# Spreading the second attention score over the partitions with two DMAs instead of TensorE transposes

## The chip, the cores and the metric

The kernel runs on one core of one Trainium2 chip. The metric is the device time of that core in microseconds (us), as the median of several runs. The kernel before takes 2290.54 us (median of 3 runs, 2290.47 to 2291.78). The span of the profiled execution is 2288.5 us. All times below that are given as a point ("at 1296.72") are microseconds from the start of that span.

## The reference, cut to what matters

`x` is 128 batch rows of 128 nodes by 512 features, `adj` is 128 by 128, everything is fp32. Four layers follow one another, each with a residual and a layer norm. The change is in layer 2, graph attention:

```python
h = jnp.einsum('bnc,cf->bnf', x, W)
a1, a2 = (a[:F_, 0], a[F_:, 0])
s1 = jnp.einsum('bnf,f->bn', h, a1)
s2 = jnp.einsum('bnf,f->bn', h, a2)
e = jax.nn.leaky_relu(s1[:, :, None] + s2[:, None, :], negative_slope=ALPHA)
e = e * mask[None, :, :]
att = jax.nn.softmax(e, axis=2)
h_prime = jnp.einsum('bij,bjf->bif', att, h)
return jax.nn.elu(h_prime + beta * h)
```

For one batch row, `s1` belongs to the node i that lies on the partitions, and `s2` to the node j that lies along the free dimension. So `s2`, which is computed with one value per partition, must be turned into a row that every partition can read. How this is done is what changes. The other layers (a graph convolution, a linear attention, an edge maximum) are not touched.

## The kernel before

**Groups and stages.** The 128 batch rows go through in 32 groups of four (`G = 4`). A group `g` passes through `layer0` to `layer3`. The large products (`r_y` in layer 0, `r_m` and `r_v` in layer 1, `r_z` in layer 2) are each made of seven block products in the order 1, 2, 6, 5, 7, 3, 4 (`ORDER`, line 287), which accumulate into three PSUM tiles, 0, 1 and 2 (`REGION`, line 288: blocks 1, 6, 7, 4 go to tile 0, block 2 to tile 1, blocks 5 and 3 to tile 2). After each block its partial sum is copied out or added out (`out` in `product`, lines 350 to 355), and the next block on the same PSUM tile has to wait until that reading is done. The reads of blocks 1, 2, 6, 5, 7, 3, 4 of `r_y` are the seven VectorE instructions `x<-r_y,x`.

**Order.** The order of the work is written by hand. Each piece of a group has a place in time in `TABLE` (in slots of 2.48 us; a group starts 28 slots after the one before), with exceptions for the last three groups in `LAST`. All pieces are sorted by this place (lines 730 and 731), and TensorE, VectorE, ScalarE and GpSimd issue their instructions in exactly that order, through the wrapper `InOrder`. So three or four groups at different stages are interleaved on each engine. The DMAs on SyncE are not held to the written order: the loads of `x` (`load`) and the stores of the output (`store`) are placed by a scheduler.

**The work around the change, for group g.**

- `dots` and `scale_dots` (VectorE) compute both scores into the small tile `d` of shape [128, 2, 4]: `d[:, 0, :]` is `s1`, `d[:, 1, :]` is `s2`. The last instruction of this is `d<-d,rstd`.
- `spread` (TensorE) makes four transposes of `d[:, 1, b]`, broadcast over 128 columns, into one PSUM bank, `p_s`. The place is 61.6, between block 3 and block 4 of the product `r_m` of the next group.
- `leaky` (VectorE) adds `p_s` and `s1` into `e` and then applies the leaky relu (`e<-e`). `weighted` (GpSimd) multiplies by `adj`, `greatest` (VectorE) takes the maximum, `exps` (ScalarE) the exponentials, `divide` the reciprocal of the sums on VectorE (`rs`) and the product on GpSimd (`e<-e,rs`), `turn_att` (TensorE) transposes into `p_eT`.
- On GpSimd, just ahead of `weighted`, stand the four instructions of `left_factors` that prepare the sums `s_y` for the product `r_y` of group g+2.
- On VectorE, the seven reads of `r_y` of group g+2 stand between and after these pieces.

Of the kernel before, what the change touches and what calls it, by code (L numbers as in the profile page):

```python
# [8 lines left out]
FP = mybir.dt.float32  # L9
# [20 lines left out]
def kernel(  # L30
# [31 lines left out]

    nc = tc.nc
    pe, dve, act, pool = (InOrder(tc, e) for e in (nc.tensor, nc.vector, nc.scalar, nc.gpsimd))
    B, N, D = x.shape
    P = 128
    assert N == P and D % P == 0
# [2 lines left out]
    G = 4  # L70
    NG = B // G
# [4 lines left out]
    work = ctx.enter_context(tc.tile_pool(name="work", bufs=1))  # L76
    small = ctx.enter_context(tc.tile_pool(name="small", bufs=4))
    psum = ctx.enter_context(tc.tile_pool(name="psum", bufs=4, space=bass.MemoryType.PSUM))

    def bank(name):  # L80
        return psum.tile([P, D], FP, tag="ps", name=name)
# [8 lines left out]
    x1, x2, x3 = {}, {}, {}  # L90

    def load(g):
        x1[g] = data.tile([P, G, D], FP, tag="x1", name=f"x1_{g}", bufs=3)
        if g == 0:
            for b in range(G):
                nc.sync.dma_start(x1[g][:, b, :], x[b])
        else:
            nc.sync.dma_start(x1[g], x[g * G : (g + 1) * G].rearrange("b n d -> n b d"))

    load(0)  # L100
    w0_sb = const.tile([P, K, D], FP)
    nc.scalar.dma_start(w0_sb, w0.rearrange("(k p) f -> p k f", p=P))
# [19 lines left out]
    ident = const.tile([P, P], FP)  # L122
# [99 lines left out]
    def each(at, f):  # L222
        for b in range(len(at)):
            emit(at[b], f, b)

    def row(at, step, n=G):
        return [at + i * step for i in range(n)]
# [6 lines left out]
        masked=[39.95], norms=[42.5], inverse=[43.1], v=row(42, 1, 7), attend=row(50.6, 1),  # L234
        residual=row(51.0, 1), dots=row(54.2, 1.1), norm1=[55.2], scale=[58.8],
        apply1=row(65.4, 0.33),
        spread=[61.6], leaky=[62.0], weighted=[63.4], greatest=[64.3], exps=[64.4],
        divide=[65.8], turn_att=[68.6], with_beta=[69.0], gather=row(71.5, 1),
        z_sums=row(75.3, 0.5), z_w=row(77, 1, 7), exp=[87.5, 88.5, 90.4, 92.0],
        elu=[87.8, 89.4, 92.8, 93.8], norm2=[95.0], apply2=row(95.7, 0.33),  # L240
# [10 lines left out]
            stats3=[27.0, 29.9, 32.2, 35.8], norm3=[42.0], apply3=row(44.0, 0.8), store=[47.4],  # L251
        ),
        NG - 2: dict(
            scale=[5.6], apply1=row(24.3, 0.8), spread=[6.9], leaky=[7.4], weighted=[9.0],
            greatest=[10.5], exps=[11.2], divide=[13.6], turn_att=[18.3], with_beta=[18.9],
            gather=row(36.7, 0.9), z_sums=row(39.95, 1.3),
            z_w=[40.0, 41.8, 43.5, 45.2, 47.0, 49.4, 51.1], exp=[51.5, 52.2, 56.2, 58.6],
            elu=row(56.9, 2.3), norm2=[66.1], apply2=row(67.7, 0.8), widen=row(73.0, 0.86),
# [7 lines left out]
            scale=[47.0], apply1=row(47.5, 0.8), spread=[48.9], leaky=[49.4], weighted=[51.0],  # L266
            greatest=[52.4], exps=row(53.2, 0.6), divide=row(53.9, 0.6),
            turn_att=row(54.4, 0.6), with_beta=row(54.9, 0.6), gather=[55.2, 56.1, 60.5, 65.0],
# [96 lines left out]
    def stats(s, g, b, t):  # L365
        if b == 0:
            s["mv"] = small.tile([P, G, 2], FP, tag="mv", name=f"mv_{g}", bufs=6)
        st = small.tile([P, 6], FP, tag="st", name=f"st_{g}_{b}")
        dve.bn_stats(st, t)
        dve.bn_aggr(s["mv"][:, b, :], st)  # L370

    def norm(at, apply_at, s, g, t):

        n = G // len(at)

        def spread(i):
            sl = slice(i * n, i * n + n)
            ve = small.tile([P, n], FP, tag=f"ve{n}", name=f"ve_{g}_{i}")
            dve.tensor_scalar(ve, s["mv"][:, sl, 1], EPS, None, op0=ALU.add)
            s["r", i] = small.tile([P, n], FP, tag=f"rstd{n}", name=f"rstd_{g}_{i}")  # L380
            pool.tensor_tensor(s["r", i], ve, mhalf[:, sl], ALU.pow)

        def shift(i):
            sl = slice(i * n, i * n + n)
            s["nm", i] = small.tile([P, n], FP, tag=f"nmean{n}", name=f"nmean_{g}_{i}")
            dve.scalar_tensor_tensor(
                s["nm", i], s["mv"][:, sl, 0], -1.0, s["r", i], op0=ALU.mult, op1=ALU.mult
            )

        def apply(b):  # L390
            i, j = b // n, b % n
            act.activation(
                t()[:, b, :],
                t()[:, b, :],
                AF.Identity,
                bias=s["nm", i][:, j : j + 1],
                scale=s["r", i][:, j : j + 1],
            )

        each(at, spread)  # L400
        for i in range(len(at)):
            emit(apply_at[i * n] - 0.1, shift, i)
        each(apply_at, apply)


    def layer0(g, t):
        s = {}

        def aggregate(b):
            if b == 0:  # L410
                s["yT"] = work.tile([P, K, G * P], FP, tag="aT_yz", name=f"yT_{g}")
            p = bank(f"p_y_{g}_{b}")
            for k in range(K):
                pe.matmul(
                    p[:, k * P : (k + 1) * P],
                    x1[g][:, b, k * P : (k + 1) * P],
                    adjT,
                    start=True,
                    stop=True,
                )  # L420
            act.copy(
                s["yT"][:, :, b * P : (b + 1) * P], p.rearrange("p (k n) -> p k n", k=K)
            )

        def biased(b):
            pool.tensor_tensor(x1[g][:, b, :], x1[g][:, b, :], bias_sb, ALU.add)

        if g > 0:
            emit(t["load"][0], load, g)
        each(t["y"], aggregate)  # L430
        each(t["bias"], biased)
        left_factors(t["y_sums"], s, "yT", "s_yz", f"y_{g}", 0)
        product(t["y_w"], f"y_{g}", by_rows, s, "0", rows_of(lambda: x1[g]), False)
        each(t["stats0"], lambda b: stats(s, f"0_{g}", b, x1[g][:, b, :]))
        norm(t["norm0"], t["apply0"], s, f"0_{g}", lambda: x1[g])
# [120 lines left out]
    s12 = {}  # L556
# [4 lines left out]
    def layer2(g, t):  # L561
        s = {}

        def spread():
            s["p"] = bank(f"p_s2_{g}")
            for b in range(G):
                pe.transpose(
                    s["p"][:, b * P : (b + 1) * P],
                    s12[g][:, 1, b : b + 1].to_broadcast([P, P]),
                    ident,  # L570
                )

        def leaky():
            e = work.tile([P, G, P], FP, tag="e", name=f"e_{g}")
            dve.tensor_tensor(
                e,
                s["p"].rearrange("p (b n) -> p b n", b=G),
                s12[g][:, 0, :, None].to_broadcast([P, G, P]),
                ALU.add,
            )  # L580
            dve.scalar_tensor_tensor(e, e, ALPHA, e, op0=ALU.mult, op1=ALU.max)
            s["e"] = e
# [89 lines left out]

        n = G // len(t["exps"])
        emit(t["spread"][0], spread)
        emit(t["leaky"][0], leaky)
        emit(t["weighted"][0], weighted)
        emit(t["greatest"][0], greatest)
# [16 lines left out]
    def layer3(g, t):  # L694
        s = {}

        def widen(b):
            s["a", b] = bank(f"p_a_{g}_{b}")
            pe.matmul(s["a", b], adjT, x3[g][:, b, :], start=True, stop=True)

        def top(b):
            x = x3[g][:, b, :]
            mx = small.tile([P, 1], FP, tag="mx", name=f"mx_{g}_{b}")
            dve.tensor_reduce(mx, s["a", b], AX.X, ALU.max)
            tp = small.tile([P, 1], FP, tag="top", name=f"top_{g}_{b}")
            dve.tensor_scalar(tp, mx, b3_sb, 0.0, op0=ALU.add, op1=ALU.max)
            act.activation(x, x, AF.Identity, bias=tp)

        def store(i):
            for b in range(i * n, i * n + n):  # L710
                nc.sync.dma_start(out[g * G + b], x3[g][:, b, :])

        n = G // len(t["store"])
        each(t["widen"], widen)
        each(t["top"], top)
        each(t["stats3"], lambda b: stats(s, f"3_{g}", b, x3[g][:, b, :]))
        norm(t["norm3"], t["apply3"], s, f"3_{g}", lambda: x3[g])
        each(t["store"], store)
# [8 lines left out]
    for g in range(NG):  # L727
        for layer in (layer0, layer1, layer2, layer3):
            layer(g, times(g))
# [31 lines left out]
```

## Time and profile before

| What | Value |
|---|---|
| time, median of 3 | 2290.54 us |
| span of the profiled execution | 2288.5 us |
| mean granted TensorE clock | 0.996 |
| ScalarE busy | 1005.3 us (44%) |
| GpSimd busy | 959.2 us (42%) |
| DMA moved | 75.21 MB, mean 33 GB/s |
| loads of `x`, 1024 KB each | 5.2 us from issue to landing |

The page gives for each engine how long it was busy, and then the chain of work that ended last: followed back from the last instruction, it says on which engine the time of the span was spent. The groups of instructions give busy time and the mean duration of one instruction, and after the last bar the time for which the engine sat idle just before them. The timeline lists single instructions with start and duration, and in brackets the idle time before them. Two neighbouring instructions of one engine overlap by about 0.1 us in it[...]. Since every group of the steady part runs the same list, its timeline repeats: the stretch from 1240 to 1314 us is used below as the example of all of them.

### The profile page before, as it was taken

Reading aid. Unit: us, or ns where it says so; the run is one execution under the profiler, and the core shown is the slowest. Engines: PE = TensorE matmul, PEld = TensorE weight load, DVE = VectorE, ACT = ScalarE, POOL = GpSimd, SP = SyncE. Lnnn points to the kernel's source line nnn. Section 1 sums busy time; section 2 is a strip of 40 time slices with the busy share of each in tenths; the row PEclk is TensorE's granted clock in tenths of the full one; section 3 lists DMA queues with packets and bytes.
Section 4 is the critical chain, followed back from the end, with each engine's and each line's share of the span. In section 5 each row is a group of like instructions: output and inputs, shape, how many; then the busy total and the mean of one; then the engine's idle time right before and its main releaser. Section 6 shows DMA issues by size and latency. Waiting matters only on the chain.

```text
span 2288.5 us, 31182 instructions
## 1 busy us (share of the span) xinstructions
PE 2250.7 (98%) x11809; PEld 1914.8 (84%) x11809; DVE 1577.0 (69%) x3319; ACT 1005.3 (44%) x1800; POOL 959.2 (42%) x775
## 2 busy tenths in 40 slices
PE   7999999999999999999999999999999999999996
PEld 5888888888888888888888888888888888888873
DVE  4656776666776667766667766667767677666677
ACT  2224444444444454444444444444444544444435
POOL 4434444344444334444344443444443344443422
PEclk9999999999999999999999999999999999999998
DMA  4000011100111100111100111001111001110001
GB/s 162 19 19 10 28 38 38 37 21 18 38 37 37 38 19 19 38 37 38 37 10 28 38 37 37 21 18 38 37 37 38 19 20 37 37 38 19 9 12 55
DMA packets 38886, 75.21 MB, mean 33 GB/s; under 512 B 3024, under 2 KB 3152, under 8 KB 38736
## 3 DMA queue, kind: packets, MB, share of 16 engines
q1 hardware_dynamic: 37536, 70.86, 8.7%
q10 hardware_dynamic: 1200, 2.36, 0.3%
q8 instruction: 93, 1.52, 0.3%
q14 instruction: 57, 0.47, 0.1%
HBM read 39.65 MB, written 33.55 MB: 32 GB/s over the span
## 4 chain that ended last, share of the span: by engine, by line
PE 94%; DVE 4%; POOL 1%; ACT 1%; issue 1%; DMA 0%; ACTq 0%; DVEq 0%; POOLq 0%
PE r_y L26 17%; PE r_v L26 16%; PE r_m L26 16%; PE r_z L26 16%; PE p_z L26 5%; PE p_rel L26 5%; PE p_o L26 5%; PE p_a L26 5%; PE p_y L26 5%; PE p_xT L26 2%; DVE x L26 1%; PE p_n L26 1%; DVE st L26 1%; PE p_eT L26 1%; PE p_m L26 1%; PE p_s L26 1%
## 5 line engine op out<-in xcount | busy, mean ns | idle before, releaser
L26 ACT ACTIVATE x<-x,nmean,rstd 128x512 f32<-128x512 f32 x512 | 386.4, 809 | 128.0 <-DVE nmean L26 127.9
L26 DVE BATCH_NORM_STATS2 st<-x 128x6 f32<-128x512 f32 x512 | 352.4, 688 | 75.3 <-ACT x L26 66.6
L26 POOL TENSOR_TENSOR rstd<-ve,mhalf 128x4 f32<-128x4 f32 (+1 forms) x134 | 144.5, 1078 | 245.3 <-DVE ve L26 241.3
L26 POOL TENSOR_TENSOR x<-x,bias_sb 128x512 f32<-128x512 f32 x128 | 174.8, 1368 | 145.5 <-PE p_y L26 145.5
L26 DVE SCALAR_TENSOR_TENSOR scr<-x,wa 128x512 f32<-128x512 f32 x256 | 214.9, 891 | 0.0
L26 ACT ACTIVATE x<-x,top 128x512 f32<-128x512 f32 x128 | 92.4, 722 | 254.1 <-DVE top L26 189.7
L26 DVE TENSOR_TENSOR x<-r_y,x 128x512 f32<-128x512 f32 x224 | 152.9, 683 | 54.4 <-PE r_y L26 44.5
L26 DVE TENSOR_TENSOR v<-r_v,v 128x512 f32<-128x512 f32 x96 | 65.8, 685 | 177.0 <-PE r_v L26 174.0
L26 POOL TENSOR_TENSOR s_x<-xT 128x512 f32<-128x512 f32 x64 | 82.2, 1285 | 222.2 <-ACT xT L26 222.2
L26 ACT COPY yT<-p_y 128x512 f32<-128x512 f32 x128 | 75.0, 586 | 206.0 <-PE p_y L26 206.0
L26 DVE SCALAR_TENSOR_TENSOR x<-p_o,rn,x 128x512 f32<-128x512 f32 x128 | 95.9, 749 | 99.5 <-PE p_o L26 96.5
L26 DVE SCALAR_TENSOR_TENSOR x<-m,x 128x512 f32<-128x512 f32 x128 | 115.1, 899 | 61.7 <-ACT m L26 51.3
L26 ACT COPY c<-r_z 128x512 f32<-128x512 f32 x124 | 72.6, 585 | 175.9 <-DVE scr L26 151.5
L26 PEld LDWEIGHTS p_y<-adjT,x 128*128 128x128 f32 x1024 | 135.3, 194 | 12.9 <-ACT adjT L26 5.0
L26 PEld LDWEIGHTS p_z<-eT,x 128*128 128x128 f32 x1024 | 135.4, 194 | 8.3 <-DVE x L26 1.2
L26 PE MATMUL p_y<-adjT,x 128*128 128x128 f32 x1024 | 136.1, 278 | 6.2 <-ACT adjT L26 4.7
L26 PEld LDWEIGHTS p_rel<-tT,xT 128*128 128x128 f32 x1024 | 134.2, 192 | 7.4 <-DVE tT L26 0.8
L26 PE MATMUL p_a<-x,adjT 128*128 128x512 f32 x256 | 133.6, 607 | 3.5 <-DVE mx L26 1.8
L26 PE MATMUL p_z<-eT,x 128*128 128x128 f32 x1024 | 136.4, 277 | 0.4 <-DVE x L26 0.4
L26 PE MATMUL p_rel<-tT,xT 128*128 128x128 f32 x1024 | 135.0, 275 | 0.6 <-DVE tT L26 0.6
L26 POOL TENSOR_TENSOR s_z<-zT 128x512 f32<-128x512 f32 x31 | 39.2, 1265 | 223.9 <-ACT zT L26 223.9
L26 PE MATMUL p_o<-v,rel 128*128 128x512 f32 x256 | 130.6, 594 | 0.0
(120 smaller groups left out, 5075.2 us busy)
## 6 DMA issues: line engine op xcount, KB each, us to landing
out_dram<-x SPq DMA_DIRECT2D x128, 256.0 KB, 2.0
x<-in_x_dram SPq DMA_DIRECT2D x31, 1024.0 KB, 5.2
w_sb<-in_L_gnn_weight_dram ACTq DMA_DIRECT2D x1, 1024.0 KB, 5.7
x<-in_x_dram SPq DMA_DIRECT2D x4, 256.0 KB, 7.5
wq_sb<-in_L_gnn_Wq_dram SPq DMA_DIRECT2D x1, 1024.0 KB, 11.7
wk_sb<-in_L_gnn_Wk_dram SPq DMA_DIRECT2D x1, 1024.0 KB, 14.6
w_sb<-in_L_gnn_W_dram ACTq DMA_DIRECT2D x1, 1024.0 KB, 10.2
wv_sb<-in_L_gnn_Wv_dram SPq DMA_DIRECT2D x1, 1024.0 KB, 13.7
```

The costliest lines, as they stand in the source:

```text
L26: return lambda *args, **kw: self.tc.keep_in_program_order(op(*args, **kw))
```

## The change: what it does and what it is for

For every group but the last, `spread` no longer runs on TensorE. Instead, the scores `s2` of the group (128 partitions by 4 values) are written by a DMA to a small tensor in DRAM, and a second DMA reads these 512 values back to every partition, as one row of 2 KB each, into the SBUF tile `wide`. `leaky` then reads this tile instead of the PSUM bank. The row holds the values with the node outside and the batch row inside (`p n b`), and `leaky` reads it as `p b n`, so along the node the reading steps over 4 values (16 bytes). The aim is to take the four transposes off TensorE. In the last group the transposes stay.

Both DMAs are issued by SyncE. All DMAs in the loop that SyncE issues (loads, the two new ones, stores) are now issued in the written order. The place of `spread` moves forward to 58.9, right behind `scale_dots` (58.8). In the group before the last (`NG - 2`) `leaky` and the pieces after it are placed later.

```diff
+    sync = InOrder(tc, nc.sync)
...
+    dram = ctx.enter_context(tc.tile_pool(name="dram", bufs=2, space=bass.MemoryType.DRAM))
...
-            nc.sync.dma_start(x1[g], x[g * G : (g + 1) * G].rearrange("b n d -> n b d"))
+            sync.dma_start(x1[g], x[g * G : (g + 1) * G].rearrange("b n d -> n b d"))
...
-        spread=[61.6], leaky=[62.0], weighted=[63.4], greatest=[64.3], exps=[64.4],
+        spread=[58.9], leaky=[62.0], weighted=[63.4], greatest=[64.3], exps=[64.4],
...
-            scale=[5.6], apply1=row(24.3, 0.8), spread=[6.9], leaky=[7.4], weighted=[9.0],
-            greatest=[10.5], exps=[11.2], divide=[13.6], turn_att=[18.3], with_beta=[18.9],
+            scale=[5.6], apply1=row(24.3, 0.8), spread=[5.7], leaky=[11.5], weighted=[13.1],
+            greatest=[14.5], exps=[15.2], divide=[17.6], turn_att=[20.9], with_beta=[21.5],
...
         def spread():
-            s["p"] = bank(f"p_s2_{g}")
-            for b in range(G):
-                pe.transpose(
-                    s["p"][:, b * P : (b + 1) * P],
-                    s12[g][:, 1, b : b + 1].to_broadcast([P, P]),
-                    ident,
-                )
+            if g == NG - 1:
...
+            else:
+                row = dram.tile([P, G], FP, tag="s2", name=f"s2d_{g}")
+                sync.dma_start(row, s12[g][:, 1, :])
+                wide = work.tile([P, P, G], FP, tag="s2", name=f"s2_{g}")
+                sync.dma_start(
+                    wide.rearrange("p n b -> p (n b)"),
+                    row.rearrange("n b -> (n b)")[None, :].to_broadcast([P, P * G]),
+                )
+                s["s2"] = wide.rearrange("p n b -> p b n")
...
             dve.tensor_tensor(
                 e,
-                s["p"].rearrange("p (b n) -> p b n", b=G),
+                s["s2"],
                 s12[g][:, 0, :, None].to_broadcast([P, G, P]),
                 ALU.add,
             )
...
-                nc.sync.dma_start(out[g * G + b], x3[g][:, b, :])
+                sync.dma_start(out[g * G + b], x3[g][:, b, :])
```

More of the change, by code (lines that the diff above doesn't have):

```diff
@@ L564, in spread @@
         def spread():
-            s["p"] = bank(f"p_s2_{g}")
-            for b in range(G):
-                pe.transpose(
-                    s["p"][:, b * P : (b + 1) * P],
-                    s12[g][:, 1, b : b + 1].to_broadcast([P, P]),
-                    ident,
+            if g == NG - 1:
+                p = bank(f"p_s2_{g}")
+                for b in range(G):
+                    pe.transpose(
+                        p[:, b * P : (b + 1) * P],
+                        s12[g][:, 1, b : b + 1].to_broadcast([P, P]),
+                        ident,
+                    )
+                s["s2"] = p.rearrange("p (b n) -> p b n", b=G)
+            else:
[5 more added lines that the diff above has]
+                    row.rearrange("n b -> (n b)")[None, :].to_broadcast([P, P * G]),
                 )
+                s["s2"] = wide.rearrange("p n b -> p b n")
         def leaky():
```

## The prediction

> **What bounds the kernel now.** I read the busy shares first, then the chain of work that ended last, then the groups that the change touches, and then one period of the timeline engine by engine.
>
> ```profile
> PE 2250.7 (98%) x11809; PEld 1914.8 (84%) x11809; DVE 1577.0 (69%) x3319; ACT 1005.3 (44%) x1800; POOL 959.2 (42%) x775
> ...
> PE 94%; DVE 4%; POOL 1%; ACT 1%; issue 1%; DMA 0%; ACTq 0%; DVEq 0%; POOLq 0%
> ...
> L26 PE MATMUL p_s<-ident,d 128*128 128x128 f32 x128 | 19.3, 273 | 2.1 <-DVE d L26 2.1
> ...
> L26 DVE TENSOR_TENSOR e<-p_s,d 128x512 f32<-128x512 f32 x32 | 21.8, 682 | 1.4 <-PE p_s L26 1.4
> ...
> out_dram<-x SPq DMA_DIRECT2D x128, 256.0 KB, 2.0
> ```
>
> TensorE is busy for 98% of the span and holds 94% of the chain: in the steady part it has no gap, so time taken off it is gained, provided that no other engine then makes it wait. The removed transposes wait for nothing in the steady part (the 2.1 us are one wait, in group 0). TensorE's timeline prices them and shows the block of `r_y` that will matter:
>
> ```profile
> 1293.76 0.60 PE L26 MATMUL p_s<-ident,d 128*128 128x128 f32 x4
> 1294.20 1.89 PE L26 MATMUL r_m<-xT,t_m 128*128 128x256 f32 x8
> ...
> 1310.30 1.89 PE L26 MATMUL r_y<-t,yT 128*128 128x256 f32 x8
> ```
>
> The next block starts 0.44 us after the transposes: that is their price. The last line is block 4 of `r_y`. It may start once VectorE has read block 7 from the same PSUM tile. VectorE and GpSimd in the same stretch:
>
> ```profile
> 1286.84 0.17 DVE L26 TENSOR_TENSOR d<-d,rstd 128x8 f32<-128x8 f32 x1
> ...
> 1296.72 0.68 DVE L26 TENSOR_TENSOR e<-p_s,d 128x512 f32<-128x512 f32 x1
> 1297.44 0.77 DVE L26 SCALAR_TENSOR_TENSOR e<-e 128x512 f32<-128x512 f32 x1
> 1298.13 0.68 DVE L26 TENSOR_TENSOR x<-r_y,x 128x512 f32<-128x512 f32 x1
> 1299.59 0.69 DVE L26 TENSOR_REDUCE nm<-e 128x4 f32<-128x512 f32 x1 [0.78 <-POOL e L26]
> ...
> 1308.68 0.69 DVE L26 TENSOR_TENSOR x<-r_y,x 128x512 f32<-128x512 f32 x1
> ```
> ```profile
> 1296.38 1.28 POOL L26 TENSOR_TENSOR s_y<-yT,s_y 128x512 f32<-128x512 f32 x1
> ...
> 1306.41 1.04 POOL L26 TENSOR_TENSOR e<-e,rs 128x512 f32<-128x512 f32 x1 [6.85 <-DVE rs L26]
> 1307.56 1.02 POOL L26 TENSOR_TENSOR rstd<-ve,mhalf 128x4 f32<-128x4 f32 x1
> ```
>
> VectorE is 69% busy on average, but from 1296 to 1309 it is full. The read of block 7 ends at 1308.68 + 0.69 = 1309.37, and block 4 starts at 1310.30: 0.93 us of room. I take 0.1 us from a VectorE end to the start of a TensorE block that waited for it: in group 0 a read ends at 122.64 and `r_y` starts at 122.79, while other waits show about 0.06. Also, `e` is added while GpSimd runs the last `s_y` sum, 1296.38 to 1297.66. I looked at this overlap in twelve periods from 185 to 2130 us; it is the same each time.
>
> **What the Trainium skill says.** (1) "SBUF — State Buffer", section "Who interferes with whom": a VectorE instruction with two SBUF inputs contends with a GpSimd instruction that reads SBUF; whichever starts first holds the shared port and the other is fully blocked, while a VectorE instruction with at most one SBUF input doesn't contend. This trace agrees. In group 0, a tensor_tensor on two SBUF inputs, 0.69 us when alone, meets a GpSimd instruction that ends at 116.56, and itself ends at 117.12, 0.56 later:
>
> ```profile
> 115.30 1.26 POOL L26 TENSOR_TENSOR yT<-yT 128x512 f32<-128x512 f32 x1
> ```
> ```profile
> 115.89 1.23 DVE L26 TENSOR_TENSOR t<-w_sb 128x512 f32<-128x512 f32 x1
> ```
>
> `d<-d,rstd`, whose second input is a broadcast, took 1.24 us instead of 0.17 in group 0, beside such a sum, and `e<-p_s,d`, with one input in PSUM, stays at 680 to 692 ns in all 32 cases. (2) The same page, "Door 1: The DMA port swizzle", notes that SBUF has lines of 16 bytes and that each access which crosses to a new line pays a penalty. It gives no figure, and the trace shows no large VectorE read of that kind. (3) "DMA: Bandwidth & Descriptors", "Anatomy of one DMA": about 2.0 us of fixed cost. The 256 KB stores land in 2.0 us, so this case agrees.
>
> **The change part by part.**
>
> *Removed from TensorE*: 31 x 4 transposes at 0.44 us for four, 13.6 us in all. In group 0 nothing is gained: TensorE stood there until 115.51 for `d`, and block 4 of `r_m` after it needs VectorE's read of block 7, which runs until 115.96. Group 30 lies in the tail, where TensorE already waits for others. So 29 groups x 0.44 = 12.8 us to be gained.
>
> *Added DMAs*: the write moves 2 KB in pieces of 16 bytes, the read 256 KB. Neither shape is in the trace. Lower bound: the 2.0 us of the stores for each, plus 0.4 us of issue (a DMA instruction takes 0.39 on SyncE), 4.8 us. Upper: for the first load of 64 KB 2.4 us were measured; twice 3 us and issue give 7. I take 5. From the end of `d` (1287.01) to `e` there are 9.7 us, so in the steady part it is hidden. In group 0 `e` starts 5.26 us after `d` ends (115.37 to 120.63): 0 to 2 us of waiting, I take 0.3.
>
> *SyncE in written order*: per group the four stores of g-2 (52.5 slots), the two new DMAs (58.9), the load of g+3 (64). The stores were issued at 1268.41 to 1272.95, before `d`. Behind the pair stands the load, issued at 1277.36 until now and some 12 us later then, but its first reader comes 20 slots, 50 us, later. The cost is nothing.
>
> *`e` reads SBUF instead of PSUM.* Now both inputs are in SBUF, and the last `s_y` sum, which started 0.34 us earlier, holds the port. By the pattern above `e` ends 0.56 after GpSimd, 1297.66 + 0.56 = 1298.22 instead of 1297.40. The next instruction `e<-e` then runs free in 0.69 instead of 0.77, so the first read of `r_y` starts at 1298.87 instead of 1298.13: **0.74 us late**. Nothing downstream gives this back: `nm<-e` waits for GpSimd's `e`, which is as late; then VectorE is full up to the reciprocal, on which GpSimd's `e<-e,rs`, then `rstd`, then `nmean`, then the read of block 7 hang.
>
> *The 16-byte step.* Bounds: 0, or every element takes twice as long. From `eT` with 128x512 (680 ns) and with 128x128 (292 ns), 384 elements cost 388 ns, so 512 cost 0.52 us more. I take the upper end, since every single element lies in a new line. VectorE is then 0.74 + 0.52 = 1.26 us late.
>
> *What that does to block 4.* It can start at 1309.37 + delay + 0.1, and a block after a wait loses about 0.1 more (2.00 instead of 1.89 us after the wait at 2210.11). Before, it started at 1310.30. So a period changes by delay - 0.73 us, never below -0.44. With 1.26: +0.53 us. Earlier blocks also wait (block 6: the read ends at 1300.07, the block would be due at 1299.83), but the last wait contains these.
>
> *Sum*: 29 x 0.53 = +15.4; group 0: 0.3 of waiting plus 0.52 for the slow read, +0.8, since `r_y` already waits there for this VectorE chain (0.43 us); tail: -0.4 for the transposes, up to +2 for `eT` placed later, I take 0. 2290.5 + 16.2 = **2306.7 us**, said as 2306.
>
> **The rivals.**
>
> A. *The port lock alone, the step of 16 bytes is free.* Delay 0.74, period +0.01: the gain of 0.44 is just eaten by the wait for block 7. 2290.5 + 29 x 0.01 + about 0.5 for the ends = 2291. For it: the page gives no size for the penalty. Against: a step that leaves no second access in a line is the case it warns of.
>
> B. *The gain arrives.* Neither lock nor step costs: 2290.5 - 12.8 + 0.5 = 2278. For it: TensorE at 98% without gaps, VectorE at 69%. Against: twelve equal overlaps of `e` with a GpSimd sum, and the long two-input instructions that I followed, which all end 0.56 us after GpSimd's. If only the step costs, `e` ends at 1296.72 + 1.20, the read is 0.44 late, a period gains 0.73 - 0.44 = 0.29, and it is 2283.
>
> C. *The DMA pair takes more than 9.7 us.* Then VectorE waits in every group, and each us adds as much to a period. Two DMAs at 2.0 us speak against it; at 11 us it would be about 1.3 x 29 = 38 us more than my forecast.
>
> **How the numbers follow.** Forecast (lock and step, wholly or in good part) 0.53, A 0.25, B with its variant 0.20, C 0.02. Slower by over 0.2% (above 2295.1) are the forecast and C, 0.54 with rounding; same is A, 0.26; faster is B, 0.20. The range reaches down to 2283, B's variant, and up to 2311: 0.15 us of latency instead of 0.1 (+1.5), 2 us in group 0, 2 us in the tail.
>
> **What would show it.** In the groups after, `e` from SBUF should average near 2.0 us (0.94 until the port is free, then 0.56 + 0.52); 1.5 says A, 0.7 says B. TensorE's waits should list `r_y` waiting for VectorE's `x` some 29 to 90 times, 20 us or more in all; the period, now 69.46 us, should be near 70.0. SyncE's waits should show the second DMA behind the first for about 2 us, and `e` waiting for a DMA at most in group 0. A DMA as the releaser of `e` in every group would make the prediction wrong, as would an `e` that overlaps `s_y` and takes 0.7 us.

## The result, and the profile after

The changed kernel takes **2303.55 us** (median of four runs, 2302.08 to 2304.05); the kernel before, beside it on the same chip, 2291.16 us (2290.47 to 2291.84). The ratio is **1.0053**, with a 95% interval of 1.0036 to 1.007: slower, by some 12 us. 2306 was forecast.

I read the page of the changed kernel in the same order as before: busy time of each engine, then the shares of the chain of waits, then the DMA issues (KB each, median us from issue to landing).

```profile
PE 2257.9 (98%) x11685; PEld 1908.1 (83%) x11685; DVE 1604.9 (70%) x3319; ACT 1006.1 (44%) x1800; POOL 959.9 (42%) x775
...
PE 89%; DVE 7%; POOL 1%; ACT 1%; issue 1%; DMA 1%; ACTq 0%; DVEq 0%; POOLq 0%
...
s<-s2d SPq DMA_DIRECT2D x31, 256.0 KB, 5.3
```

TensorE has 124 instructions fewer and is nevertheless "busy" for 7 us more: in the modelled busy time, short waits inside a run of matmuls don't show as gaps. Its share of the chain falls from 94% to 89%, and VectorE's rises from 4% to 7%. That is where the forecast looked for it. VectorE's group for `e` (count, then the shortest, median and longest in ns, then the first and last start):

```profile
L26 DVE TENSOR_TENSOR e<-s,d x31: 1055/1786/1796, 122.0 to 2206.9; 128x512 f32<-128x512 f32 x31
```

It was 680 to 692 ns before. The same stretch of a period as in the prediction, on GpSimd and VectorE of the changed kernel (start, duration, both in us), and last the `tT` of the kernel before, to measure from:

```profile
1304.36 1.27 POOL L26 TENSOR_TENSOR s_y<-yT,s_y 128x512 f32<-128x512 f32 x1
```
```profile
1304.12 0.66 DVE L26 TENSOR_TENSOR tT<-r_m,tT 128x512 f32<-128x512 f32 x1
1304.70 1.79 DVE L26 TENSOR_TENSOR e<-s,d 128x512 f32<-128x512 f32 x1
1306.52 0.69 DVE L26 SCALAR_TENSOR_TENSOR e<-e 128x512 f32<-128x512 f32 x1
1307.13 0.68 DVE L26 TENSOR_TENSOR x<-r_y,x 128x512 f32<-128x512 f32 x1
...
1317.62 0.16 DVE L26 SCALAR_TENSOR_TENSOR nmean<-mv,rstd 128x4 f32<-128x4 f32 x1 [1.13 <-POOL rstd L26]
1317.70 0.69 DVE L26 TENSOR_TENSOR x<-r_y,x 128x512 f32<-128x512 f32 x1
```
```profile
1296.15 0.66 DVE L26 TENSOR_TENSOR tT<-r_m,tT 128x512 f32<-128x512 f32 x1
```

`e` starts 0.34 us after the `s_y` sum and ends 0.86 us after it (1306.49 against 1305.63); in all 28 periods it is 0.86. The first read of `r_y` starts 3.01 us after `tT` started, where before it was 1.98: VectorE is **1.03 us late**. At the read of block 7 (the last line) it is still 1.05 late, 13.58 us after `tT` instead of 12.53: nothing in between gave it back. TensorE in the same stretch, and below it the kernel before:

```profile
1306.92 1.05 PE L26 MATMUL p_rel<-tT,xT 128*128 128x128 f32 x8
1307.96 1.97 PE L26 MATMUL r_y<-t,s_y 128*128 128x256 f32 x8
...
1315.00 1.05 PE L26 MATMUL p_rel<-tT,xT 128*128 128x128 f32 x8
1316.00 1.97 PE L26 MATMUL r_y<-w_sb,s_y 128*128 128x256 f32 x8
1317.80 0.60 PE L26 MATMUL p_eT<-ident,e 128*128 128x128 f32 x4
1318.44 1.99 PE L26 MATMUL r_y<-t,yT 128*128 128x256 f32 x8
```
```profile
1299.38 1.05 PE L26 MATMUL p_rel<-tT,xT 128*128 128x128 f32 x8
1300.27 1.89 PE L26 MATMUL r_y<-t,s_y 128*128 128x256 f32 x8
...
1309.86 0.60 PE L26 MATMUL p_eT<-ident,e 128*128 128x128 f32 x4
```

Three blocks of `r_y` start late, and are recognised by the start of the line before them and by their own duration. An `r_y` block follows a `p_rel` block after 0.89 us where nothing is awaited (1299.38 to 1300.27 before); the first of the three now comes after 1.04, the second after 1.00, and the last, block 4, comes 0.64 after `p_eT` instead of 0.44. Each of them then takes 1.97 to 1.99 instead of 1.89. The waits are 0.15 + 0.10 + 0.20 in the median of all groups, and by the start of what follows them the slower blocks cost 0.07 + 0.07 + 0.10: 0.70 us a period. The transposes gave 0.44, which leaves 0.26. From one `d` to the next (28 periods, groups 1 to 29) the median period went from 69.46 to 69.72 us, **+0.26**: the sum is the measured one. The average went from 69.462 to 69.749, +0.288, because two of the 28 periods are longer than the others by 0.35.

The profiled spans differ by 13.5 us (2288.5 and 2302.0). By the starts of `d`: 28 periods bring +8.04, the stretch from group 0 to group 1 +3.40 (61.33 to 64.73), and the rest from group 29 to the end +2.03 (168.11 to 170.14).

**Group 0.** Waits in brackets:

```profile
122.04 1.05 DVE L26 TENSOR_TENSOR e<-s,d 128x512 f32<-128x512 f32 x1 [1.28 <-DMA s<-s2d]
```
```profile
124.57 2.98 PE L26 MATMUL r_y<-t,s_y 128*128 128x256 f32 x8 [2.17 <-DVE x L26]
```
```profile
124.50:127.30 2.80, 2.73 (x8) 2.26 (x9) 1.35 (x3) 1.38 (x7) 0.67 (x1) 0.66 0.00 0
127.30:129.00 1.70, 1.70 (x10) 1.66 (x9) 0.78 (x2) 1.70 (x5) 0.50 (x1) 0.56 0.00 0
```

`e` waits 1.28 us for the read from DRAM. The `r_y` block behind it waits 2.17 us instead of 0.43 and then takes 2.98 us. The last fence is the table by stretch (length, busy us and instructions of the five engines, granted TensorE clock, DMA share, GB/s): over the 4.5 us after the wait the granted clock is 0.66 and 0.56 of full speed in the mean, and 0.50 from 125.4 to 128.7. That is 2.80 x 0.34 + 1.70 x 0.44 = 1.7 us lost, and with the 1.74 us of longer waiting it makes up the 3.40.

**The end** also has a longer wait with a lower clock behind it (0.50 from 2217.8 to 2224.5). No DMA is waited for here: the pieces of group 30 that the change placed later now stand ahead of `rel` on VectorE, from which GpSimd makes `sq`:

```profile
2216.93 1.16 PE L26 MATMUL p_n<-ones,sq 128*128 128x1 f32 x8 [3.01 <-POOL sq L26]
2219.67 1.11 PE L26 MATMUL p_eT<-ident,e 128*128 128x128 f32 x4 [1.59 <-POOL e L26]
```
```profile
2217.00:2220.50 3.50, 1.91 (x12) 1.83 (x13) 2.10 (x6) 0.00 (x0) 1.93 (x2) 0.61 0.02 5
2220.50:2226.00 5.50, 5.50 (x18) 4.48 (x17) 0.97 (x4) 3.99 (x6) 1.08 (x2) 0.63 0.00 0
```

### The profile page after: what moved, and what is told of

The parts are those of the page before. It is cut to its first block, busy times and chain, and to the rows that moved or that the text cites. A ratio compares the mean times of both kernels' runs of the same rounds, so it can differ in the third digit from the quotient of the medians.

```text
span 2302.0 us, 30995 instructions
## 1 busy us (share of the span) xinstructions
PE 2257.9 (98%) x11685; PEld 1908.1 (83%) x11685; DVE 1604.9 (70%) x3319; ACT 1006.1 (44%) x1800; POOL 959.9 (42%) x775
## 4 chain that ended last, share of the span: by engine, by line
PE 89%; DVE 7%; POOL 1%; ACT 1%; issue 1%; DMA 1%; ACTq 0%; DVEq 0%; POOLq 0%
PE r_v L26 16%; PE r_z L26 16%; PE r_m L26 15%; PE r_y L26 15%; PE p_z L26 5%; PE p_y L26 5%; PE p_a L26 5%; PE p_o L26 5%; PE p_rel L26 4%; DVE x L26 2%; PE p_xT L26 2%; DVE st L26 1%; PE p_n L26 1%; DVE e L26 1%; PE p_m L26 1%
```

## The experiments

The **theory**: `e` with two SBUF inputs is held by the port that GpSimd uses, and the 16-byte step of `s2` adds to it; VectorE's chain is late, and the late reads of `r_y` hold TensorE by more than the transposes gave. **Rivals**: the DMA pair, or the written order of SyncE, is what costs; or the steady part is no worse, and the ends are. Expectations are quoted as they were written ahead of each run. The first four kernels share a median of the kernel before of 2290.59 us, the last four one of 2291.56.

### 1. The row in DRAM turned, so that `e` reads packed elements

```
-row = dram.tile([P, G], ...)
-sync.dma_start(row, s12[g][:, 1, :])
-wide = work.tile([P, P, G], ...)
+row = dram.tile([G, P], ...)
+sync.dma_start(row.rearrange("b n -> n b"), s12[g][:, 1, :])
+wide = work.tile([P, G, P], ...)
...
-s["s2"] = wide.rearrange("p n b -> p b n")
+s["s2"] = wide
```

> The changed kernel, but the row in DRAM is written with the batch row outside and the node inside, so that the tile is read with neighbouring values (no 16-byte step); the write DMA then moves pieces of 4 bytes. Theory (port lock plus step plus the chain to the read of block 7): e still waits for the s_y sum, ends 0.56 us after it, so about 1.5 us long instead of 1.79; VectorE is 0.74 late instead of 1.03; the period falls from 69.72 to about 69.45 us, as long as before the change; time about 2295 us. Rival (the step costs nothing, the lock alone makes e 1.79 long): e stays at 1.79, time 2303. Rival (the DMAs cost): the write with 4-byte pieces is slower, so e waits for a DMA and the time is above 2303.

Measured: 2464.55 us, ratio 1.076 (1.0745 to 1.0775). The theory's number missed by 170 us. DMA issues, then VectorE's waits (us in all, times, longest), then the group of `e`:

```profile
s2d<-d SPq DMA_DIRECT2D x31, 2.0 KB, 8.4
```
```profile
DVE e L26 <- DMA s<-s2d: 157.5, 31, 9.6
```
```profile
L26 DVE TENSOR_TENSOR e<-s,d x31: 691/692/694, 130.2 to 2366.7; 128x512 f32<-128x512 f32 x31
```

The write now goes out in pieces of 4 bytes instead of 16, and lands in 8.4 us instead of 1.4. With the read (6.0) the pair passes the 9.7 us of room, and `e` waits in every group; the mean period is 74.77 us. This is what the prediction's rival C would have looked like, and it shows by contrast that the pair of the changed kernel, which holds `e` only in group 0, is not the cost in the steady part. The run was meant to price the step and does so in another way: `e` comes so late here that no `s_y` sum runs beside it, and it takes 0.692 us. In group 0 of the changed kernel, also with no sum beside it, it takes 1.055; in group 0 of run 8, packed and without a sum, 0.680. The 16-byte step costs 0.36 us for 512 elements, 0.71 ns each.

### 2. The read of block 7 ahead of `nmean`

```
-apply2=row(95.7, 0.33)
+apply2=row(95.85, 0.33)
```

The read no longer stands behind `nmean`, which waits for GpSimd's `rstd`.

> The changed kernel, with one place in the written order moved: VectorE's read of block 7 of r_y stands ahead of nmean of layer 2, no longer behind it, so it doesn't hang on GpSimd's e<-e,rs and rstd. Theory: the wait of block 4 (0.20 us and 0.10 of restart) goes, those of blocks 6 and 3 stay; e stays at 1.79 us; the period falls by about 0.30 to 69.42 us; time about 2295 us. Rival (what costs is the DMA pair or e itself, not the chain to block 7): unchanged, 2303.

Measured: 2295.15 us, ratio 1.0019 (1.0011 to 1.0026). `e` still takes 1.785 us, and the period is 69.42 us: 0.3 us less than in the changed kernel, for moving one read on VectorE by the length of one wait. Block 4 doesn't wait any more (0.44 after `p_eT`), while blocks 6 and 3 wait as in the changed kernel. What set the period there is this read, not `e`'s own length.

### 3. One input of `e` in PSUM again

ScalarE copies the first scores (128x4) into a PSUM tile, and `e` takes its broadcast input from there; `s2` stays in SBUF with its step.

```
+p1 = bank(f"p_s1_{g}")
+act.copy(p1[:, :G], s12[g][:, 0, :])
+s["s1"] = p1[:, :G]
...
-s12[g][:, 0, :, None].to_broadcast([P, G, P]),
+s["s1"][:, :, None].to_broadcast([P, G, P]),
```

> The changed kernel, with s1 copied by ScalarE (128x4) into a PSUM bank that the change had freed, so that e has only one input in SBUF; the step of 16 bytes stays. Theory (port lock): e no longer waits for GpSimd and takes about 1.05 us, as in the two groups where no sum runs beside it; VectorE is about 0.3 late instead of 1.03, which is less than the room that block 4 has; TensorE has no wait in the steady part and the period is 69.02 to 69.1 us; time about 2284 us. Rival (no lock, the DMA-written tile is slow to read in itself): e stays at 1.79 and the time at 2303.

Measured: 2283.13 us, ratio 0.9967 (0.9954 to 0.9979). VectorE and GpSimd of this kernel:

```profile
1293.01 1.08 DVE L26 TENSOR_TENSOR e<-s,p_s 128x512 f32<-128x512 f32 x1
```
```profile
1292.66 1.27 POOL L26 TENSOR_TENSOR s_y<-yT,s_y 128x512 f32<-128x512 f32 x1
```

The overlap is the same, but `e` runs through in 1.08 us instead of 1.79. The DMAs, the order of SyncE and the step are all still there; what went is the second SBUF input. VectorE is 0.33 us late. Without the transposes block 4 is due 0.44 earlier, so 0.93 - 0.44 = 0.49 us of its room are left, which is enough: no block of `r_y` waits, and the period is 69.03 us. Nearly the whole 0.44 of the transposes is gained. The total gains less than 29 x 0.44 because the two ends stay long (63.67 and 169.60 us).

### 4. TensorE's old work put back

Four transposes a group at the old place, in groups 0 to 29; nothing reads their result, and `e` uses the DMA's row as before.

```
+if g < NG - 2:
+    emit(28.0 * g + 61.6, idle_turns)
```

> The changed kernel with the four transposes put back at their old place in groups 0 to 29, their result unread: the DMA path and the extra TensorE work together. Theory (block 4 of r_y starts when VectorE has read block 7, not when TensorE is free): the 0.44 us of TensorE fall into waits that are there anyway; the period stays at 69.7 us within 0.1, time 2300 to 2306 us. Rival (TensorE's own work sets the period, and the loss comes from elsewhere): 29 x 0.44 us more, 2316 us.

Measured: 2303.72 us, ratio 1.0056 (1.0043 to 1.0068); mean period 69.746 us, against 69.749 in the changed kernel. Blocks 6 and 3 now start without a wait, block 4 still waits (0.16 us), and it is as late as before: 0.44 us of TensorE work a group costs nothing. In this stretch TensorE has that much slack, and the end of the stretch is VectorE's.

### 5. The ends as before

Group 0 and group 30 with the transposes at their old places and times, the DMA pair in groups 1 to 29 only.

```
-if g == NG - 1:
+if g == 0 or g >= NG - 2:
```

> The changed kernel with the old transposes, at their old places, in group 0 and in the group before the last; the DMAs stay in groups 1 to 29. Theory (the loss is the sum of a slow steady part and of two losses at the ends): the steady period stays at 69.73 us, group 0 and the tail go back to those of the kernel before: 2290.5 + 29 x 0.28 = about 2298.7 us. Rival (the ends cost nothing, all of the 13 us lies in the period): 2303.

Measured: 2298.57 us, ratio 1.0028 (1.0017 to 1.0038), so about 5 us of the loss are in the ends. The period stays at 69.73. Group 0 to 1 takes 62.34 us (64.73 after), group 29 to the end 166.1 (170.14 after).

Neither end is quite that of the kernel before, and the forecast was met partly by luck. The tail is 2 us shorter: the kernel before has a stretch of lower clock in its own tail (0.71 between 2245.38 and 2250.38 us), which this run has not, nor has run 8 (166.4 us), whose last two groups run as they do before. Group 0 is 1.0 us longer: `p_s` waits 2.09 us there, as it does before (2.10), but here the granted clock is 0.50 from 116.7 to 120.0 us, and before it is 1.00. So the same wait is followed by a lower clock in one kernel and not in the other; its length alone doesn't decide.

### 6. Runs 3 and 5 together

> The changed kernel with s1 in PSUM in groups 1 to 29 (one SBUF input, no port lock) and with the old transposes in group 0 and in the group before the last. Theory (TensorE's work is the bound once VectorE isn't late): the period is 69.03 us, the ends are those of before, and the 29 x 0.43 us arrive: about 2278 us. Rival (the DMA path costs something in each period that is not seen yet): 2281 us or more.

Measured: **2277.41 us** (2276.47 to 2277.88), ratio 0.9938 (0.9925 to 0.995): faster than the kernel before by 14 us and than the changed one by 26. Mean period 69.049 us, ends 61.34 and 165.4. 28 x 0.41 = 11.6 us of it are the steady part. The tail gives 2.7, of which some 1.7 are the lower clock in the tail of the kernel before, which isn't the change's doing. This is the change as it can be used: the gain was there, behind the port lock.

### 7. SyncE's order

Loads and stores issued as before, only the two new DMAs in written order; the load of 1 MB then stands ahead of the pair instead of 0.4 us behind it.

```
-sync.dma_start(x1[g], x[g * G : (g + 1) * G].rearrange("b n d -> n b d"))
+nc.sync.dma_start(x1[g], x[g * G : (g + 1) * G].rearrange("b n d -> n b d"))
```

(and the same for the stores)

> The changed kernel with loads and stores no longer held to the written order; only the two new DMAs are. The load of 1024 KB then stands ahead of the pair and not right behind it. Theory (the second DMA lands late, 5.3 us, because the load that is issued 0.4 us after it shares the DMA engines): it lands in 2 to 2.5 us, group 0 no longer waits for it and keeps its clock, about 3 us less in group 0; the steady period stays at 69.73; time about 2300.5 us. Rival (5.3 us is what the read to all partitions from one row costs): landing 5 us, time 2303.

Measured: 2299.95 us, ratio 1.0039 (1.0025 to 1.0053). DMA issues and group 0 of this kernel:

```profile
s<-s2d SPq DMA_DIRECT2D x31, 256.0 KB, 4.0
```
```profile
123.50 1.97 PE L26 MATMUL r_y<-t,s_y 128*128 128x256 f32 x8 [1.23 <-DVE x L26]
```
```profile
124.50:130.00 5.50, 5.50 (x35) 5.06 (x34) 2.55 (x6) 4.47 (x12) 1.04 (x1) 1.00 0.00 1
```

The read lands in 4.0 us in the median, not in the 2 to 2.5 that I expected without the load behind it: 4.0 is the read itself, and 1.3 was the load's. In group 0, `e` waits 0.31 us instead of 1.28. Less than half of this difference is the read's (4.18 us instead of 4.62). The rest is the write's (1.41 instead of 1.94), which in the changed kernel had landed before the load was issued, so the order doesn't explain it. TensorE waits 1.23 us instead of 2.17, and the granted clock stays at 1.00. Group 0 to 1 takes 62.13 us. The median period is as it was, so the order costs nothing there. The 3.6 us are 2.6 in group 0, of which 1.7 are the clock's, and about 1 of other things: this run has no long single periods (0.7) and a tail shorter by 0.4.

### 8. The lock alone

In the kernel before, ScalarE copies the transposed scores from PSUM into a packed SBUF tile, which `e` reads: two SBUF inputs, no step, no DMA, in groups 0 to 29.

```
+s["w"] = work.tile([P, G, P], ...)
+act.copy(s["w"], s["p"].rearrange("p (b n) -> p b n", b=G))
...
-s["p"].rearrange("p (b n) -> p b n", b=G),
+s["w"] if g < NG - 2 else s["p"].rearrange("p (b n) -> p b n", b=G),
```

> The kernel before, transposes included, but in groups 0 to 29 ScalarE copies the PSUM bank of the second scores into a packed SBUF tile, and e reads that: two SBUF inputs, no 16-byte step, no DMA. Theory (lock alone): e waits for the s_y sum and takes about 1.5 us instead of 0.68, VectorE is 0.74 late, which is within the 0.93 us of room that block 4 has when the transposes stay: period 69.46 to 69.5, time 2290 to 2292 us. Rival (no lock; the 16-byte step and the DMA make e long): e takes 0.69 us, time 2290.5.

Measured: 2291.14 us, ratio 1.0 (0.9992 to 1.0008).

```profile
L26 DVE TENSOR_TENSOR e<-s,d x30: 680/1476/1489, 120.9 to 2131.1; 128x512 f32<-128x512 f32 x30
```

`e` takes 1.476 us and ends 0.55 us after GpSimd's sum; VectorE is 0.72 us late, and the median period is 69.46, as without the copy. The lock alone uses up most of the 0.93 us of room and costs nothing while the transposes are there.

## Why the prediction was right, and where its terms were off

**Right, and shown.** The direction, and the way: `e` is held by the port (runs 3 and 8), VectorE's lateness passes undiminished to the read of block 7 (1.03 at the first read, 1.05 there), and that read sets the period (runs 2 and 4). The port lock was forecast as 0.74 us late and measured as 0.72. The rule that a period changes by the delay less 0.73 us, never below -0.44, holds within 0.04 us for the three delays that were measured (median periods):

| kernel | VectorE late, us | rule | period change |
|---|---|---|---|
| changed | 1.03 | +0.30 | +0.26 |
| run 3 | 0.33 | -0.40 | -0.43 |
| run 8, transposes still there | 0.72 | 0 at least | 0.00 |

It is a little high because of the 0.1 us from a VectorE end to the start of a waiting block: for block 4 it was 0.05 (1318.39 to 1318.44), for blocks 6 and 3 0.15.

The Trainium skill, "SBUF — State Buffer", "Who interferes with whom", carried this, and the runs agree on both halves of it: 1.48 us with two SBUF inputs in packed form, 1.09 us with one, the latter with the step and with the same sum beside it.

**The 16-byte step was mis-sized.** I took the upper bound, 0.52 us; it is 0.36 by itself (group 0 against run 1), and 0.31 as added delay beside the lock (1.03 - 0.72). The delay was therefore 1.03 instead of 1.26, and the steady part cost 29 x 0.29 = 8.4 us by the mean period instead of 15.4. The Trainium skill, "SBUF — State Buffer", "Door 1: The DMA port swizzle", named the penalty without a size; half way between the bounds would have been nearer.

**Group 0 was mis-sized**, +3.4 instead of +0.8, half of it longer waiting and half the lower clock. The failing step is the DMA pair: 5 us were taken, and in group 0 it took 6.6, still inside the bounds of 4.8 to 7. The write was a little faster than the 2.0 us of a store (1.94 there, 1.4 in the median), the read slower (4.62 there, 5.3 in the median): a store's 2.0 us was no price for a row that goes to 128 partitions. "The cost is nothing" of SyncE's order failed with it, if by less: the order puts the load behind the read, which adds 1.3 us to it in the median and 0.4 in group 0. That TensorE's clock can be lower after a wait, 1.7 us here, stands in no step of the prediction.

**The tail was mis-sized**, about +1.75 (the 2.03 less one longer period) instead of 0, and this is still too little: the kernel before lost some 1.7 us in its own tail to a lower clock, and against run 5, which has none, the changed kernel's tail is 4.0 us longer. The term that failed is the `eT` placed later, taken at 0 with up to 2. The waits for `sq` and `e` are 3.0 and 1.6 us, and the clock is at 0.50 for 6.7 us behind the first. How the 4.0 us divide between waits and clock isn't separated.

So 16.2 us were forecast, 15.4 of them in the steady part, and 13.5 came in the profiled span, 8.4 of them there: two errors of opposite sign. That the total came within some 3 us is in part luck. **The rivals:** A describes run 8, lock without step; the changed kernel with a free step was not tried. B's arrival is run 6. C is run 1.

**The signs.** `e` "near 2.0 us" came at 1.79, nearer to it than to the 1.5 of rival A. The first DMA holds SyncE for 1.2 us in the mean (38.3 us in 31 groups), not 2. `e` waits for a DMA once (last line below), in group 0. A poor sign was that TensorE's waits should list `r_y` waiting for `x` with 20 us or more in all (us in all, times, longest):

```profile
PEld r_y L26 <- DVE x L26: 8.5, 29, 0.6
...
PE r_y L26 <- DVE x L26: 2.8, 3, 2.2
...
DVE e L26 <- DMA s<-s2d: 1.3, 1, 1.3
```

The first line has the 29 periods but only 0.3 us each: most of the loss lies in waits of 0.1 to 0.2 us that the modelled ends of the matmuls swallow. Starts compared between two kernels show them.

**Open:** single periods that are longer than the others by 0.3 to 0.4 us (70.09 among 69.72), two in the changed kernel and one or two in six of the experiments. In the changed kernel one VectorE instruction starts 0.35 us late in each; what it waits for doesn't show. Open too is what decides whether a wait of TensorE is followed by a lower clock.

## What to carry to other kernels

When an input of a VectorE instruction moves from PSUM to SBUF, look in the timeline at what GpSimd does beside that instruction, not at its duration: here 0.4 us of saved TensorE work turned into a loss through an add that became 1.1 us longer, and one small copy to PSUM turned it back. A saved piece of work is worth at most what the next engine leaves of its room in that stretch; measure the room (0.93 us here) and what the change takes of it (1.03) before counting the saving. And count the ends of the program apart: here they had no slack, and 5 of the 12 us were lost there.

## What the runs showed of the hardware

- A write of 2 KB to DRAM landed in 1.4 us as 128 pieces of 16 bytes and in 8.4 us as 512 pieces of 4 (medians). Whether the size of the pieces or their number makes the difference was not tried.
- A row of 2 KB read from DRAM to all 128 partitions took 4.0 us, where a store of 256 KB, in as many pieces of 2 KB, lands in 2.0; with a load of 1 MB issued 0.4 us behind it, 5.3.
- A step of 16 bytes in one fp32 input of a VectorE add cost 0.36 us for 512 elements (0.692 to 1.055 us): dearer, but not double.
- A VectorE add with two SBUF inputs that began 0.34 us after a GpSimd sum ended 0.55 us after it (run 8), and 0.86 us after it with the 16-byte step; with one of the inputs in PSUM it took 1.09 us with the step and was not held (run 3).
- In group 0, a TensorE wait of 2.1 us was followed by a granted clock of 0.50 for some 3.4 us in run 5, but not in the kernel before. After one of 2.17 us the clock fell in the changed kernel; after one of 1.23 us in the same place it stayed at 1.00 (run 7). In the tail, a wait of 3.0 us was followed by 0.50 for 6.7 us. Which length is enough was not found.
- A block of eight matmuls took 1.97 to 2.00 us after a short wait and 1.89 without one.
